# Grouping the part-array matmuls of a two-layer graph network kernel into two stretches per group

## The chip, the core and the metric

The kernel runs on one core of a Trainium2 chip. Five engines work beside each other, each through its own list of instructions in order: TensorE (PE; its weight loads are shown as PEld), VectorE (DVE), ScalarE (ACT), GpSimd (POOL) and SyncE (SP), which here only starts DMAs. ScalarE and GpSimd start DMAs as well. Engines wait for each other through semaphores. The metric is the device time of one execution in microseconds (us).

## The reference

Two layers over a batch of 128 graphs, each with 128 nodes and 512 features; everything is float32.

```python
# layer 0: h = relu(layernorm(x))
q, k, v = h @ Wq.T, h @ Wk.T, h @ Wv.T
rel = adjacency.T[None] * einsum('bnd,bmd->bnm', q, k)
rel = rel / norm(rel, axis=2, keepdims=True)
x = x + einsum('bnm,bmd->bnd', rel, v)
# layer 1: h = relu(layernorm(x)), 8 heads of 64
q, k, v = (h @ Wq + bq), (h @ Wk + bk), (h @ Wv + bv)      # as [b, n, 8, 64]
scores = einsum('bihd,bjhd->bhij', q, k) / 8 + where(adj == 0, -1e9, 0)
x = x + einsum('bhij,bjhd->bihd', softmax(scores), v)
```

## The kernel before

The batch is cut into 32 groups of four graphs (numbered 0 to 3 in a group). A group goes through layer 0, then layer 1. Layer 0 needs two products with weights (G, in which Wq and Wk are merged, and V), layer 1 three (Q, K, V). Each is a (512 x 512) by (512 x 512) product done by Strassen's scheme in the form with seven multiplications, and class `Product` holds its seven steps P1 to P7. One step is eight matmul passes on TensorE (`mm`, L225) into one of three PSUM banks x, y, z, and then one operation that takes the result out of the bank: `keep` or `copy` on ScalarE (on VectorE for layer 1's V), `add` on VectorE. P6, P7 and P4 add onto bank x, and P3 onto bank z, so each waits until the step before it has been copied out of that bank.

All engines follow an order written out by hand: lists of steps (`FIRST`, `SECOND`, `ORDER`, `LAST`) which `run` goes through. `ORDER` is used for thirty of the groups. The letter ahead of the point says whose step it is: `l` is layer 1 of the group in work, `m` layer 0 of the next, `n` layer 1 of that next group, `f` layer 0 of the one after, `p` layer 1 of the group before `l`. So while `l` is multiplied, `m` and the rest of `p` run beside it. Each step appends instructions to the lists of the engines it uses; an engine never does a later step's instruction ahead of an earlier one's.

The steps that the change touches:

- `S(b)` (L459): the scores of graph b, eight heads of 64 rows each, so a matmul uses half of the array's rows and two run side by side. They go to the two banks `pss` (pool `ps_s`) or, for b = 1, to two banks `pso` of pool `ps_o`. `mk(b)` adds the mask and takes the negative row maximum on VectorE (L484, L489); `ex(b)` does eight exponentials on ScalarE and sends the weights to a scratch buffer in DRAM (L191). `mkA`, `mkB`, `exC`, `exD` are the same in two halves, for scores that lie in two `pso` banks.
- `wr(b)` fetches the weights back in blocks with four DMAs of SP (L199), `wt(b)` transposes them within blocks on VectorE (L511) and takes the reciprocal of the sums.
- `A(i)` (L619): the outputs of graphs 2i and 2i+1, matmuls that write 64 of the 128 partitions. `oc(i)` copies them out on ScalarE and sends them, `rdo(i)` fetches them, `ot(i)` transposes and scales them and adds them to the output in DRAM with two DMAs of POOL (L661). "First outputs" are A(0), "second outputs" A(1).
- `N` (L411): the norm sums of layer 0, matmuls that write 32 partitions each. They need `mask_rel` (VectorE) and `square` (ScalarE) of the result of `R`.
- `hn(i)` normalises two graphs on ScalarE (L308) and sends them (512 KB), `rd(i)` fetches them with SP, `T(i)` transposes them on VectorE (L320). `T(0)` makes the operand of P1 and P2, `T(1)` and the sums `sumA`, `sumB` those of the other steps.
- `O(b)` and `xO(b)`: layer 0's outputs on TensorE, then scaled and added to x on VectorE; `stat` and `inv` (VectorE, POOL) make the statistics for layer 1's `hn`.
- `load`, `sto`: x comes in (POOL) and goes out (SP).

Part-array matmuls are those of S, N and A; all others use the whole array. Buffers: `tpool` holds two fetched tiles u, `scratch` four DRAM buffers of each kind, `ppool` one tile for tag `pgv`, which gT (from G) and layer 1's v share.

Of the kernel before, what the change touches and what calls it, by code (L numbers as in the profile page):

```python
# [9 lines left out]
F32 = mybir.dt.float32  # L10
# [4 lines left out]
P = 128  # L15
G = 4
# [5 lines left out]
def kernel(  # L22
# [28 lines left out]
    ppool = ctx.enter_context(tc.tile_pool(name="ppool", bufs=1))  # L51
    rpool = ctx.enter_context(tc.tile_pool(name="rpool", bufs=4))
    npool = ctx.enter_context(tc.tile_pool(name="npool", bufs=3))
    tpool = ctx.enter_context(tc.tile_pool(name="tpool", bufs=2))
    wpool = ctx.enter_context(tc.tile_pool(name="wpool", bufs=3))
    work = ctx.enter_context(tc.tile_pool(name="work", bufs=2))
    small = ctx.enter_context(tc.tile_pool(name="small", bufs=8))
    scratch = ctx.enter_context(
        tc.tile_pool(name="scratch", bufs=4, space=bass.MemoryType.DRAM)
    )  # L60
    ps_mm = ctx.enter_context(tc.tile_pool(name="ps_mm", bufs=4, space=PSUM))
    ps_s = ctx.enter_context(tc.tile_pool(name="ps_s", bufs=1, space=PSUM))
# [139 lines left out]
    class Product:  # L202
# [7 lines left out]
            self.bias, self.name, self.ps, self.r = bias, name, {}, {}  # L210

        def quarter(self, i, j):
            if self.turned:
                return self.dest[:, 2 * j : 2 * j + 2, i * HF : (i + 1) * HF]
            return self.dest[:, 2 * i : 2 * i + 2, j * HF : (j + 1) * HF]

        def mm(self, bank: str, w: int, xs, first: bool):
            if first:
# [154 lines left out]
    class Layer0(Layer):  # L373
        n = 0

        def start(self):
            g = self.g
            self.gT = ppool.tile([P, KD, G * P], F32, tag="pgv", name=f"gT_{g}")
            self.v = ppool.tile([P, G, D], F32, tag="pv0", name=f"v0_{g}")
            self.po = {}  # L380
            self.G = Product(self, "a", self.gT, True, name=f"pg_{g}")
            self.V = Product(self, "v0", self.v, False, name=f"pv0_{g}")

        def R(self):

            pr = ps_o.tile([P, G, P], F32, tag="po", name=f"pr_{self.g}")
            for b in range(G):
                for k in range(KD):
                    nc.tensor.matmul(  # L389
                        pr[:, b, :], lhsT=self.turned(k, b), rhs=self.gT[:, k, ts(b, P)],  # L390
                        start=(k == 0), stop=(k == KD - 1),
                    )
            self.pr = pr
# [43 lines left out]
    class Layer1(Layer):  # L437
# [15 lines left out]
                nc.sync.dma_start(out[self.g * G + b], x_tiles.pop((self.g, b)))  # L453

        def start_v(self):
            self.v = ppool.tile([P, G, D], F32, tag="pgv", name=f"v1_{self.g}")
            self.V = Product(self, "v1", self.v, False, bv_sb, name=f"pv1_{self.g}")

        def S(self, b):  # L459
            g = self.g  # L460

            if b == 1 or (b == 3 and g == NG - 1):
                half = [ps_o.tile([P, NH, P], F32, tag="po", name=f"pso_{g}_{r}") for r in range(2)]
            else:
                pss = ps_s.tile([P, 2, NH, P], F32, tag="ps", name=f"pss_{g}_{b}")
                half = [pss[:, r] for r in range(2)]
                self.ps[b] = pss.rearrange("p r k j -> p (r k) j")
            self.half_s[b] = half
            for k in range(NH):
                for r in range(2):  # L470
                    rows = slice(r * HD, (r + 1) * HD)
                    nc.tensor.matmul(  # L472
                        half[r][:, k, :],
                        lhsT=self.qT[rows, k, ts(b, P)], rhs=self.kT[rows, k, ts(b, P)],
                        start=True, stop=True,
                    )
# [94 lines left out]
        def An(self, b):  # L571

            wT, self.po[b] = self.wT.pop(b), []
            parts = 2 if b == G - 1 else 1
            n = NH // parts
            for t in range(parts):
                pool, tag = (ps_mm, "mm") if b % 2 else (ps_o, "po")
                po = pool.tile([P, 2 * n * HD], F32, tag=tag, name=f"pn1_{self.g}_{b}_{t}")
                for k in range(n):
                    for r in range(2):  # L580
                        i = 2 * (t * n + k) + r
                        nc.tensor.matmul(
                            po[:, ts(2 * k + r, HD)], lhsT=wT[:, r * NH + t * n + k, :],
                            rhs=self.v[:, b, ts(i, HD)], start=True, stop=True,
                        )
                self.po[b].append(po)

# [31 lines left out]
        def A(self, i):  # L619


            for b in range(2 * i, 2 * i + 2):
                wT = self.wT.pop(b)
                po = ps_o.tile([P, NH, P], F32, tag="po", name=f"po1_{self.g}_{b}")
                for k in range(NH):
                    for r in range(2):
                        nc.tensor.matmul(  # L627
                            po[r * HD : (r + 1) * HD, k, :],
                            lhsT=self.v[:, b, ts(2 * k + r, HD)], rhs=wT[:, r * NH + k, :],
                            start=True, stop=True,  # L630
                        )
                self.po[b] = po
# [39 lines left out]
    """.split()  # L672
    SECOND = """
        l.Q.P1 l.sumA l.Q.P2 l.sumB l.K.P1 l.K.P2 l.Q.P5 l.Q.P6 l.sto0 l.sto1 f.load0 f.load1 l.Q.P3 l.K.P5 l.K.P6 l.Q.P7
        l.K.P3 l.K.P7 l.S0 l.mk0 f.load2 f.load3 l.Q.P4 l.K.P4 l.ex0 l.wr0 m.V.P1 f.stat0 f.stat1 f.inv0
        m.V.P2 m.V.P5 m.R m.mask_rel m.square f.stat2 f.stat3 f.inv1 m.V.P6 l.S1 m.N l.S2 l.mkA1 m.norms l.exC1
        l.mkB1 l.exD1 l.wr1 l.wt0 m.V.P3 l.add_mask2 m.V.P7 m.O0 m.xO0 m.O1 m.xO1 n.stat0 n.stat1 n.inv0
        m.V.P4 l.mx2 n.hn0 n.rd0 l.exC2 l.exD2 l.wr2 l.start_v l.V.P1 m.O2 m.xO2 m.O3 m.xO3 n.stat2 n.stat3 n.inv1
        l.V.P2 l.wt1 l.V.P5 n.hn1 n.rd1 l.V.P6
        l.V.P3 n.T0 l.V.P7 l.S3 l.A0 l.mk3 l.oc0 l.wt2 l.V.P4 l.ex3 n.T1 n.start  # L680
    """.split()
    ORDER = """
        l.Q.P1 p.rdo0 l.sumA l.Q.P2 p.wr3 m.hn0 l.sumB l.K.P1 m.rd0 l.K.P2 p.ot0 l.Q.P5 l.Q.P6 m.hn1 m.rd1
        l.sto0 l.sto1 l.Q.P3 l.Q.P7 p.wt3 m.T0 l.K.P5 l.K.P6 l.Q.P4 f.load0 f.load1 l.K.P3
        l.K.P7 m.T1 m.sumA m.sumB m.start m.G.P1 l.K.P4 m.G.P2 l.S0 p.A1 l.mk0 p.oc1 p.rdo1 m.G.P5 m.G.P6
        l.ex0 l.wr0 m.G.P3 m.V.P1 m.G.P7 p.ot1 m.V.P2 f.stat0 f.stat1 f.inv0 m.G.P4 m.V.P5
        l.wt0 f.load2 f.load3 m.R m.mask_rel m.square m.V.P6 l.S1 m.N l.S2 l.mkA1 m.norms l.exC1 l.mkB1 l.exD1
        l.wr1 m.V.P3 l.add_mask2 m.V.P7 m.O0 m.xO0 m.O1 m.xO1 n.stat0 n.stat1 n.inv0 m.V.P4 l.mx2
        n.hn0 n.rd0 l.exC2 l.exD2 l.wr2 l.start_v l.V.P1 m.O2 m.xO2 m.O3 m.xO3 n.stat2 n.stat3 n.inv1
        l.V.P2 l.wt1 l.V.P5 n.hn1 n.rd1 l.V.P6 f.stat2 f.stat3 f.inv1  # L690
        l.V.P3 n.T0 l.V.P7 l.S3 l.A0 l.mk3 l.oc0 l.wt2 l.V.P4 l.ex3 n.T1 n.start
    """.split()
    LAST = """
        l.Q.P1 p.rdo0 l.sumA l.Q.P2 p.wr3 l.sumB l.K.P1 l.K.P2 p.ot0 l.Q.P5 l.Q.P6 l.Q.P3 p.wt3 l.K.P5 l.K.P6
        p.A1 p.oc1 p.rdo1 l.K.P3 l.Q.P7 l.S0 l.mk0 l.K.P7 l.ex0 l.wr0 l.Q.P4 p.ot1 l.K.P4 l.S1 l.mkA1 l.exC1
        l.start_v l.V.P1 l.mkB1 l.exD1 l.wr1 l.V.P2 l.wt0 l.V.P5 l.S2 l.S3 l.add_mask2 l.V.P6 l.mx2 l.exA2 l.exB2
        l.mkA3 l.exA3 l.V.P3 l.V.P7 l.tw2 l.wt1 l.mkB3 l.exB3 l.V.P4 l.An0 l.fin0 l.An1 l.fin1 l.tw3 l.An2 l.fin2
        l.An3 l.fin3
    """.split()
# [1 line left out]
    def run(order, **who):  # L701
        for step in order:
            name, *path = step.split(".")
            at = who.get(name)
            if at is None:
                continue
            if len(path) == 2:
                getattr(getattr(at, path[0]), path[1])()
            elif path[0][-1].isdigit():
                getattr(at, path[0][:-1])(int(path[0][-1]))  # L710
            else:
                getattr(at, path[0])()

    with tc.manual_schedule(engines={EN.PE, EN.SP, EN.Pool, EN.DVE, EN.Activation}):
        p, l, m = None, None, Layer0(0)
        for b in range(G):
            m.stat(b)
        m.inv(0)
        m.inv(1)
        for b in range(G):  # L720
            load(1, b, nc.gpsimd)
        load1()
        m.hn_pe(0)
        m.hn_pe(1)
        f = Layer0(1)
        weights0(lambda: m.turn_pe(0))
        m.turn_pe(1)
        weights_v0()
        for g in range(NG):
            n = Layer1(g)  # L730
            if g:
                f = Layer0(g + 1) if g + 1 < NG else None
            run((FIRST, SECOND, ORDER)[min(g, 2)], p=p, l=l, m=m, n=n, f=f, w=Weights1())
            p, l, m = l, n, f
        run(LAST, p=p, l=l)


# [28 lines left out]
```

## Time and profile before

| What | us |
|---|---|
| median of 3 runs (2489.47 to 2493.50) | 2490.89 |
| the profiled execution | 2492.48 |
| its span, from first to last instruction | 2490.6 |
| TensorE's granted clock in the span | 0.999 of full speed |

| one group, 1281.77 to 1358.32 | busy us |
|---|---|
| TensorE matmul | 76.55 of 76.55 |
| TensorE weight load | 65.53 |
| VectorE | 52.48 |
| ScalarE | 31.73 |
| GpSimd | 12.49 |
| DMA engines, mean busy share | 0.64 |

A timeline row gives the start, the length, the engine, the source line, the operation, the tile written and those read, shapes and the number of instructions; in brackets, how long the engine was idle before it and what released it. Matmuls overlap in the pipeline, so rows of TensorE are to be read from start to start and not by their lengths. "ACTq", "SPq" are DMAs that the engine issues. The DMA rows end with the median time in us from issue to landing.

### The profile page before, as it was taken

Reading aid. Unit: us, or ns where it says so; the run is one execution under the profiler, and the core shown is the slowest. Engines: PE = TensorE matmul, PEld = TensorE weight load, DVE = VectorE, ACT = ScalarE, POOL = GpSimd, SP = SyncE. Lnnn points to the kernel's source line nnn. Section 1 sums busy time; section 2 is a strip of 40 time slices with the busy share of each in tenths; the row PEclk is TensorE's granted clock in tenths of the full one; section 3 lists DMA queues with packets and bytes.
Section 4 is the critical chain, followed back from the end, with each engine's and each line's share of the span. In section 5 each row is a group of like instructions: output and inputs, shape, how many; then the busy total and the mean of one; then the engine's idle time right before and its main releaser. Section 6 shows DMA issues by size and latency. Waiting matters only on the chain.

```text
span 2490.6 us, 40700 instructions
## 1 busy us (share of the span) xinstructions
PE 2480.6 (100%) x14688; PEld 2114.1 (85%) x14688; DVE 1686.6 (68%) x2549; ACT 1028.4 (41%) x3248; POOL 417.3 (17%) x820
## 2 busy tenths in 40 slices
PE   9999999999999999999999999999999999999999
PEld 7888888888888888888888888888888888888887
DVE  5666776666766677766677666676667776667766
ACT  3344443444433444434444344443444443344434
POOL 5111111111111111111111111111111111111110
PEclk9999999999999999999999999999999999999999
DMA  5366655676655766556665566665566655666555
GB/s 188 114 182 191 194 164 167 174 196 181 181 167 168 196 182 182 175 162 180 195 186 170 166 173 197 184 169 169 169 196 186 178 169 163 193 192 181 177 146 134
DMA packets 396408, 438.21 MB, mean 176 GB/s; under 512 B 31600, under 2 KB 289008, under 8 KB 396208
## 3 DMA queue, kind: packets, MB, share of 16 engines
q1 hardware_dynamic: 297376, 201.22, 29.8%
q10 hardware_dynamic: 70000, 165.96, 18.2%
q0 software_dynamic: 28832, 68.44, 13.3%
q8 instruction: 116, 1.90, 0.3%
q14 instruction: 84, 0.69, 0.1%
HBM read 204.80 MB, written 230.69 MB: 175 GB/s over the span
## 4 chain that ended last, share of the span: by engine, by line
PE 93%; DMA 2%; DVE 1%; ACT 1%; issue 1%; SPq 0%; POOL 0%; ACTq 0%; DVEq 0%; POOLq 0%
PE pv_x L225 16%; PE pg_x L225 9%; PE pv_z L225 9%; PE pq_x L225 8%; PE pk_x L225 8%; PE pg_z L225 5%; PE pr L389 5%; PE po L627 4%; PE pq_z L225 4%; PE pk_z L225 4%; PE pv_y L225 4%; PE po L429 4%; PE pss L472 4%; PE pg_y L225 2%; PE pk_y L225 2%; PE pq_y L225 2%
## 5 line engine op out<-in xcount | busy, mean ns | idle before, releaser
L225 PE MATMUL pv_x<-wc_v,h 128*128 128x256 f32 x1280 | 300.6, 382 | 0.1
L320 DVE STREAM_TRANSPOSE h<-u_h 128x1024 f32<-128x1024 f32 x126 | 156.8, 1245 | 187.7 <-DMA u_h<-d_h 185.0
L225 PEld LDWEIGHTS pv_x<-wc_v,h 128*128 128x128 f32 x1280 | 240.4, 190 | 50.8 <-issue 19.5
L661 POOL DMA_DIRECT2D out_dram<-o x124 | 111.8, 901 | 1013.5 <-DVE o L654 1010.5
L225 PE MATMUL pv_z<-wc_v,s 128*128 128x256 f32 x1024 | 245.2, 382 | 0.3 <-DVE pv_r L242 0.3
L308 ACT ACTIVATE hn<-xb,shift,rstd 128x512 f32<-128x512 f32 x252 | 191.5, 810 | 74.6 <-POOL shift L300 57.4
L225 PEld LDWEIGHTS pv_z<-wc_v,s 128*128 128x128 f32 x1024 | 191.8, 190 | 29.3 <-DVE pv_r L242 0.7
L496 ACT ACTIVATE e<-pss,nmax 128x128 f32<-128x128 f32 x504 | 177.7, 381 | 42.7 <-DVE nmax L489 42.7
L225 PE MATMUL pv_x<-wc_v,s 128*128 128x256 f32 x768 | 181.7, 379 | 0.0
L225 PE MATMUL pq_x<-h,wc_q 128*128 128x256 f32 x768 | 181.5, 379 | 0.0
L225 PE MATMUL pk_x<-h,wc_k 128*128 128x256 f32 x768 | 181.5, 379 | 0.0
L638 ACT COPY oT<-po 128x512 f32<-128x512 f32 x124 | 72.8, 587 | 259.0 <-PE po L627 181.1
L290 DVE BATCH_NORM_STATS2 st<-xb 128x6 f32<-128x512 f32 x256 | 172.2, 673 | 8.3 <-DMA xb<-in_x_dram 8.3
L511 DVE STREAM_TRANSPOSE wT<-u_w 128x1024 f32<-128x1024 f32 x126 | 152.8, 1213 | 29.2 <-DMA u_w<-d_w 28.5
L225 PEld LDWEIGHTS pk_x<-h,wc_k 128*128 128x128 f32 x768 | 145.8, 190 | 19.9
L225 PEld LDWEIGHTS pq_x<-h,wc_q 128*128 128x128 f32 x768 | 145.8, 190 | 19.9
L225 PEld LDWEIGHTS pv_x<-wc_v,s 128*128 128x128 f32 x768 | 143.3, 190 | 18.4 <-issue 0.2
L70 POOL DMA_DIRECT2D xb<-in_x_dram x124 | 73.3, 593 | 365.7 <-DMA out_dram<-xb 227.8
L225 PE MATMUL pq_z<-s,wc_q 128*128 128x256 f32 x512 | 122.0, 381 | 2.5 <-DVE qT L249 2.4
L225 PE MATMUL pg_z<-s,wc_a 128*128 128x256 f32 x512 | 124.1, 385 | 0.0
L225 PE MATMUL pg_x<-h,wc_a 128*128 128x256 f32 x512 | 121.0, 379 | 1.1 <-DVE h L320 1.1
L627 PE MATMUL po<-wT,v 128*64 128x128 f32 x1984 | 122.0, 276 | 0.0
(156 smaller groups left out, 4690.8 us busy)
## 6 DMA issues: line engine op xcount, KB each, us to landing
d_h<-hn ACTq DMA_DIRECT2D x126, 512.0 KB, 4.3
u_h<-d_h SPq DMA_DIRECT2D x504, 128.0 KB, 3.6
d_w<-e ACTq DMA_DIRECT2D x126, 512.0 KB, 3.1
u_w<-d_w SPq DMA_DIRECT2D x504, 128.0 KB, 3.4
out_dram<-xb SPq DMA_DIRECT2D x126, 256.0 KB, 3.2
xb<-in_x_dram POOLq DMA_DIRECT2D x124, 256.0 KB, 3.0
d_o<-oT ACTq DMA_DIRECT2D x62, 512.0 KB, 3.8
u_o<-d_o SPq DMA_DIRECT2D x248, 128.0 KB, 3.2
```

What stands on the lines that cost most here:

```text
L70: queue.dma_start(xb, x[g * G + b])
L225: nc.tensor.matmul(ps[:, m, :], lhsT=lhsT, rhs=rhs, start=first and m == 0 and k == 0, stop=k == 1, skip_group_check=True,)
L290: nc.vector.bn_stats(st, x_tiles[g, b])
L308: nc.scalar.activation(hn[:, r], x_tiles[g, b].rearrange("p (k j q) -> p j k q", j=TB, q=BK), AF.Relu, bias=self.shift[:, b : b + 1], scal ...
L320: nc.vector.transpose(half.rearrange("p k (t i) -> p t k i", i=BK), self.u.pop(i).rearrange("p t (k q) -> p t k q", q=BK),)
L389: nc.tensor.matmul(pr[:, b, :], lhsT=self.turned(k, b), rhs=self.gT[:, k, ts(b, P)], start=(k == 0), stop=(k == KD - 1),)
L429: nc.tensor.matmul(po, lhsT=self.rel[:, b, :], rhs=self.v[:, b, :], start=True, stop=True)
L472: nc.tensor.matmul(half[r][:, k, :], lhsT=self.qT[rows, k, ts(b, P)], rhs=self.kT[rows, k, ts(b, P)], start=True, stop=True,)
L496: nc.scalar.activation(e[:, :, i, :], sc[:, i, :].rearrange("p (j q) -> p j q", q=BK), AF.Exp, bias=nmax[:, i : i + 1], accum_out=self.tot ...
L511: nc.vector.transpose(self.wT[b].rearrange("p h (t i) -> p t h i", i=BK), self.uw.pop(b).rearrange("p t (h q) -> p t h q", q=BK),)
L627: nc.tensor.matmul(po[r * HD : (r + 1) * HD, k, :], lhsT=self.v[:, b, ts(2 * k + r, HD)], rhs=wT[:, r * NH + k, :], start=True, stop=True,)
L661: nc.gpsimd.dma_start(out[g * G + b], o.rearrange("p k t q -> p (k t q)"), accum_op=ALU.add)
```

## The change

The part-array matmuls of a group stood in three places: S0 with the second outputs of the group before; S1, N and S2; S3 with the first outputs. They now stand in two: second outputs (A1), S0, S1, N; and S2, S3, first outputs (A0). For that

- S3 uses two `pso` banks in every group, and its mask and exponentials come in halves at the start of the next group (`p.mkA3 p.mkB3 p.exC3 p.exD3`); scores 2 take the place at the group's end (`l.mk2`, `l.exC2 l.exD2 l.wr2`), scores 0 come behind scores 1;
- the outputs go to banks of `ps_mm` instead of `ps_o`;
- gT and layer 1's v are cut into halves, with three half buffers for both, since v's second half now lives until after R of the next group;
- V's steps come in the order P1, P2, P6, then (behind the stretch) P5, P7, P3, P4, and V.P4 stands ahead of O0;
- the fetch and the last step of the second outputs (`o.rdo1`, `o.ot1`) come a group later, so a group before `p` is kept as `o`; `tpool` has three buffers and `scratch` eight;
- `wr0` stands right ahead of `n.rd0`, `rdo0` behind `oc0`, and `f.load2 f.load3` with the statistics earlier.

```diff
-    tpool = ctx.enter_context(tc.tile_pool(name="tpool", bufs=2))
+    tpool = ctx.enter_context(tc.tile_pool(name="tpool", bufs=3))
...
-        tc.tile_pool(name="scratch", bufs=4, space=bass.MemoryType.DRAM)
+        tc.tile_pool(name="scratch", bufs=8, space=bass.MemoryType.DRAM)
...
         def quarter(self, i, j):
-            if self.turned:
-                return self.dest[:, 2 * j : 2 * j + 2, i * HF : (i + 1) * HF]
-            return self.dest[:, 2 * i : 2 * i + 2, j * HF : (j + 1) * HF]
+            a, c = (j, i) if self.turned else (i, j)
+            if isinstance(self.dest, list):
+                return self.dest[a][:, :, c * HF : (c + 1) * HF]
+            return self.dest[:, 2 * a : 2 * a + 2, c * HF : (c + 1) * HF]
...
-            self.gT = ppool.tile([P, KD, G * P], F32, tag="pgv", name=f"gT_{g}")
+            self.gT = [
+                ppool.tile([P, 2, G * P], F32, tag="pgv", bufs=3, name=f"gT_{g}_{j}") for j in range(2)
+            ]
...
-            self.v = ppool.tile([P, G, D], F32, tag="pgv", name=f"v1_{self.g}")
+            self.v = [
+                ppool.tile([P, 2, D], F32, tag="pgv", bufs=3, name=f"v1_{self.g}_{i}") for i in range(2)
+            ]
...
-            if b == 1 or (b == 3 and g == NG - 1):
+            if b % 2:
                 half = [ps_o.tile([P, NH, P], F32, tag="po", name=f"pso_{g}_{r}") for r in range(2)]
...
         def A(self, i):
+            pool, tag = (ps_o, "po") if i and self.g == NG - 2 else (ps_mm, "mm")
             for b in range(2 * i, 2 * i + 2):
                 wT = self.wT.pop(b)
-                po = ps_o.tile([P, NH, P], F32, tag="po", name=f"po1_{self.g}_{b}")
+                po = pool.tile([P, NH, P], F32, tag=tag, name=f"po1_{self.g}_{b}")
...
     ORDER = """
-        l.Q.P1 p.rdo0 l.sumA l.Q.P2 p.wr3 m.hn0 l.sumB l.K.P1 m.rd0 l.K.P2 p.ot0 l.Q.P5 l.Q.P6 m.hn1 m.rd1
-        l.sto0 l.sto1 l.Q.P3 l.Q.P7 p.wt3 m.T0 l.K.P5 l.K.P6 l.Q.P4 f.load0 f.load1 l.K.P3
-        l.K.P7 m.T1 m.sumA m.sumB m.start m.G.P1 l.K.P4 m.G.P2 l.S0 p.A1 l.mk0 p.oc1 p.rdo1 m.G.P5 m.G.P6
-        l.ex0 l.wr0 m.G.P3 m.V.P1 m.G.P7 p.ot1 m.V.P2 f.stat0 f.stat1 f.inv0 m.G.P4 m.V.P5
-        l.wt0 f.load2 f.load3 m.R m.mask_rel m.square m.V.P6 l.S1 m.N l.S2 l.mkA1 m.norms l.exC1 l.mkB1 l.exD1
-        l.wr1 m.V.P3 l.add_mask2 m.V.P7 m.O0 m.xO0 m.O1 m.xO1 n.stat0 n.stat1 n.inv0 m.V.P4 l.mx2
-        n.hn0 n.rd0 l.exC2 l.exD2 l.wr2 l.start_v l.V.P1 m.O2 m.xO2 m.O3 m.xO3 n.stat2 n.stat3 n.inv1
-        l.V.P2 l.wt1 l.V.P5 n.hn1 n.rd1 l.V.P6 f.stat2 f.stat3 f.inv1
-        l.V.P3 n.T0 l.V.P7 l.S3 l.A0 l.mk3 l.oc0 l.wt2 l.V.P4 l.ex3 n.T1 n.start
+        l.Q.P1 p.mkA3 l.sumA m.hn0 l.Q.P2 p.mkB3 p.exC3 l.K.P1 l.sumB m.rd0 p.exD3 p.wr3 l.K.P2 p.ot0 l.Q.P5 p.wt2 l.Q.P6
+        m.hn1 m.rd1 l.sto0 l.sto1 l.Q.P3 l.Q.P7 m.T0 l.K.P5 l.K.P6 p.wt3 l.Q.P4 o.rdo1 f.load0 f.load1 l.K.P3
+        l.K.P7 m.T1 m.sumA m.sumB m.start m.G.P1 l.K.P4 m.G.P2 f.load2 f.load3 m.V.P1 m.G.P5 m.G.P6 o.ot1
+        m.G.P3 f.stat0 f.stat1 f.inv0 m.G.P7 m.V.P2 f.stat2 f.stat3 f.inv1 m.G.P4 m.V.P6 m.R m.mask_rel p.A1 m.square
+        l.S0 p.oc1 l.S1 m.N l.mkA1 m.norms m.V.P5 l.exC1 l.mkB1 m.V.P7 l.exD1 l.wr1 l.add_mask0 m.V.P3 l.mx0
+        m.V.P4 l.ex0 l.wr0 m.O0 m.xO0 m.O1 m.xO1 n.stat0 n.stat1 n.inv0 n.hn0 n.rd0 l.start_v l.V.P1 m.O2 m.xO2 m.O3 m.xO3
+        n.stat2 n.stat3 n.inv1 l.V.P2 l.V.P5 n.hn1 n.rd1 l.wt1 l.V.P6
+        l.V.P3 l.wt0 l.V.P7 n.T0 l.S2 l.S3 l.A0 l.mk2 l.oc0 l.rdo0 l.V.P4 l.exC2 l.exD2 l.wr2 n.T1 n.start
     """.split()
```

`SECOND` (one group) has the same two stretches, without the steps of `p` and `o`. `LAST` (layer 1 of the last group) gets the steps of scores 3 at its start and puts A1 next to S0:

```diff
     LAST = """
-        l.Q.P1 p.rdo0 l.sumA l.Q.P2 p.wr3 l.sumB l.K.P1 l.K.P2 p.ot0 l.Q.P5 l.Q.P6 l.Q.P3 p.wt3 l.K.P5 l.K.P6
-        p.A1 p.oc1 p.rdo1 l.K.P3 l.Q.P7 l.S0 l.mk0 l.K.P7 l.ex0 l.wr0 l.Q.P4 p.ot1 l.K.P4 l.S1 l.mkA1 l.exC1
...
+        l.Q.P1 l.sumA l.Q.P2 p.mkA3 l.sumB l.K.P1 p.exC3 p.mkB3 l.K.P2 p.exD3 p.wr3 p.ot0 l.Q.P5 o.rdo1 l.Q.P6 p.wt2 l.Q.P3
+        l.K.P5 l.K.P6 l.K.P3 p.wt3 l.Q.P7 p.A1 l.S0 p.oc1 p.rdo1 o.ot1 l.mk0 l.K.P7 l.ex0 l.wr0 l.Q.P4 p.ot1 l.K.P4 l.S1 l.mkA1 l.exC1
...
```

## The prediction

> **What bounds the kernel now.** The page's table of engines comes first, then the chain that ended last.
>
> ```profile
> PE 2480.6 (100%) x14688; PEld 2114.1 (85%) x14688; DVE 1686.6 (68%) x2549; ACT 1028.4 (41%) x3248; POOL 417.3 (17%) x820
> PE 93%; DMA 2%; DVE 1%; ACT 1%; issue 1%; SPq 0%; POOL 0%; ACTq 0%; DVEq 0%; POOLq 0%
> ```
>
> TensorE is never without work, so its own order and pace are the time. The groups repeat, so I read one on the timeline, from Q.P1 at 1203.85 us to the next at 1281.77. I call the start of Q.P1 zero. Q.P1 of the third group starts at 129.61 and that of the last stage at 2432.06: thirty groups in 2302.45, 76.75 each. The commonest length, with no wait in it, is 76.55. So waits cost 0.20 a group (late sums or transposes before Q.P5 and G.P1), and TensorE's own work is 76.55.
>
> TensorE's rows around one part-array stretch, and two neighbouring score blocks that the last stage already has:
>
> ```profile
> 1229.39 1.89 PE L225 MATMUL pk_x<-h,wc_k 128*128 128x256 f32 x8
> 1231.12 1.89 PE L225 MATMUL pg_y<-h,wc_a 128*128 128x256 f32 x8
> 1232.94 1.16 PE L472 MATMUL pss<-kT,qT 64*128 64x128 f32 x16
> 1234.03 1.97 PE L627 MATMUL po<-wT,v 128*64 128x128 f32 x32
> 1235.93 1.99 PE L225 MATMUL pg_z<-s,wc_a 128*128 128x256 f32 x8
> 1237.76 1.89 PE L225 MATMUL pg_x<-s,wc_a 128*128 128x256 f32 x8
> ...
> 2466.18 1.16 PE L472 MATMUL pss<-kT,qT 64*128 64x128 f32 x16
> 2467.18 1.06 PE L472 MATMUL pso<-kT,qT 64*128 64x128 f32 x16
> 2468.16 1.99 PE L225 MATMUL pv_x<-wc_v,s 128*128 128x256 f32 x8
> ```
>
> Read start to start. A product takes 1.73; one followed by a stretch 1.82 (1231.12 to 1232.94); one that follows a stretch 1.83 (1235.93 to 1237.76). Scores alone take 1.09, outputs A 1.90, norms N 0.36 (1256.33 to 1256.69). Two score blocks in a row take 1.98, not 2.18: a change of shape costs about 0.1 on each side of the border.
>
> ScalarE at the start of a group:
>
> ```profile
> 1203.60 0.37 ACT L496 ACTIVATE e<-pss,nmax 128x128 f32<-128x128 f32 x1 [0.88 <-DVE nmax L489]
> ...
> 1206.54 0.34 ACTq L191 DMA_DIRECT2D d_w<-e  x1
> 1206.93 0.84 ACT L236 ACTIVATE pq_r<-pq_x,bq_sb 128x256 f32<-128x256 f32 x2 [0.42 <-ACT e L496]
> 1207.65 1.51 ACT L308 ACTIVATE hn<-xb,shift,rstd 128x512 f32<-128x512 f32 x2
> 1209.20 0.37 ACTq L191 DMA_DIRECT2D d_h<-hn  x1
> 1209.61 0.84 ACT L236 ACTIVATE pk_r<-pk_x,bk_sb 128x256 f32<-128x256 f32 x2 [0.44 <-PE pk_x L225]
> 1212.68 0.84 ACT L236 ACTIVATE pq_r<-pq_z,bq_sb 128x256 f32<-128x256 f32 x2 [2.23 <-PE pq_z L225]
> ```
>
> Eight exponentials and their send, Q.P1's copy, the pair hn0 and its send, K.P1's copy, then Q.P5's copy, for which ScalarE waited 2.23 us on TensorE. Its average of 41% hides that this stretch is nearly full.
>
> **The change, part by part.**
>
> *Fewer borders.* Before, a group has S0+A, S1+N+S2 and S3+A: 3 x 0.09 into them, 4 x 1.09, 2 x 1.90, 0.36, 3 x 0.10 out: 9.09. After (compiled order): A,S0,S1,N and S2,S3,A: 2 x 0.09, 2 x 1.98, 2 x 1.90, 0.36, 2 x 0.10: 8.50. That is 0.59 less, a floor of 75.96. A product to A is not new: the last stage has it at 2445.87, 2447.69 and 2449.59, 1.82 and 1.90 again.
>
> [...]
>
> *Scores 3 move into the next group's start.* Before, A waited on S3 next to it, and p.mk3 and p.ex3 ran at the group's end; now p.mk2 and exC2/exD2 run there, and p.mkA3, mkB3, exC3, exD3 follow in the next group. Nothing is computed twice, but ScalarE now has sixteen exponentials before Q.P5's copy instead of eight. Q.P3 adds onto the PSUM bank z that Q.P5 filled, so TensorE cannot start it before that copy (L258, L264). Queued behind Q.P3 is everything that TensorE has, so each late microsecond is one of the group. The chain:
>
> 1. O0 to the group's end: 20.43 before (1261.34 to 1281.77). V.P4 moves ahead of O0 (-1.73) and S2 comes in (1.98-1.09 = +0.89): 19.59.
> 2. O0 to the send of the first half, through xO, the statistics, POOL and hn0: 7.56 (1261.34 to 1268.90), the same steps in the same order: send at -12.03.
> 3. Send to transpose n.T0 (the lag): 8.27 in this group, between 8.3 and 9.2 over thirty groups, middle one 8.54.
>
> ```profile
> 1268.90 0.38 ACTq L191 DMA_DIRECT2D d_h<-hn  x1
> 1271.75 2.04 SPq L199 DMA_DIRECT2D u_h<-d_h  x4
> 1277.17 1.25 DVE L320 STREAM_TRANSPOSE h<-u_h 128x1024 f32<-128x1024 f32 x1 [0.69 <-DMA u_h<-d_h]
> d_h<-hn ACTq DMA_DIRECT2D x126, 512.0 KB, 4.3
> ```
>
> 4. T0 to the first exponential of scores 2: 1.17 to the next VectorE instruction, 1.25 mask, 1.22 maximum, 0.04: 3.68.
> 5. ScalarE without a gap: 2.94 (eight exponentials) + 0.39 + 0.72 (Q.P1) + 1.55 (hn0) + 0.41 + 1.40 (exC3) + 0.72 (K.P1) + 1.54 (exD3) + 0.40 + 0.84 (Q.P5) = 10.91; the four-exponential times are those of scores 1 (1257.94, 1259.49, send 1261.03). And 0.05 to TensorE.
>
> With a lag of 8.54 the copy is done at -12.03+8.54+3.68+10.96 = 11.15. Q.P3 is due after six products, at 10.36. So even with the lag of before it is 0.79 late, which pays back all of the 0.59 and the 0.20.
>
> The lag itself is not kept. Wr0 now stands on SP just ahead of n.rd0, and its fetch is in flight while the 512 KB of hn0 are sent; before, this send went alone and SP saw it landed after 2.85. Sends into a running fetch are in the trace too: the other half of the layer-1 input (7.44 before the group's end) took some 4 to 5.7, and m.hn0 beside the fetch of u_o 4.1 to 4.4. A send of 4.2 makes the lag 9.9. The page's median of all such sends, 4.3, says the same. Lower end: 2.85 + 1.5 of issues + 3.6 (median landing of u_h) = 7.95, if the fetch also gains because scores 2 no longer send at that moment. I take 9.2, between the lag of before and the crowded one, because the two overlap only in part: Q.P3 1.45 late.
>
> [...]
>
> *What else moves.* The second half: send at -8.3; its path before took 9.7 to 12.2, 10.5 in the middle, so n.T1 at 1.4 to 2.3, seldom 3.9. Then mkA3 and the sums stand before Q.P2's add: 1.17+0.73+0.61+0.73+0.61+0.68 = 4.53, so 5.9 to 6.8 against Q.P5 at 6.91. Covered, but nearly used up; a later one falls into the same wait at Q.P3. mk3 in two halves costs VectorE 2 x 1.34 instead of 2.40, beside TensorE. *At nothing:* A into the banks of ps_mm (its successors Q.P2, K.P1 and V.P5 wait for oc, done 1 us or more before); S1 into the other two banks (mask_rel is done 2 us before); gT and v1 in three half buffers, three fetch buffers, eight scratch buffers (space, no instruction); o.rdo1 and l.rdo0 on SP, four issues of some 0.45 each, SP idle from 22.5 to 35.7 before (they would cost if n.rd1 stood behind them; it stands ahead); f.load2/f.load3 earlier on POOL and o.ot1 with its two output DMAs a group later (POOL idles 10.6 and 16.6 us in front of these; the loads need 3.0 and the statistics come over 4 later); wt0 just before A (data about 1 us early, A would pay if the fetch took that longer); m.square before oc (0.6 of ScalarE, V.P5 has 2 us left).
>
> *Ends.* The second group gains 0.59, too. The last stage joins A and S0 (-0.2) and gets the same exponentials ahead of Q.P5's copy without hn0 (0 to +1.7): +0.6 taken. Together nothing.
>
> **Sum.** Thirty groups x (75.96 + late - 76.75). At 1.45 late: 30 x 0.66 = +20. The profiled execution took 2492.48 with a span of 2490.6; the runs' median is 2490.89, so I add to that: **2511 us**.
>
> **Rivals.**
> - *A, faster:* the traffic that leaves (scores 2's send and fetch, before beside this fetch) outweighs the one that comes. Place: n.rd0. Lag 7.95: late 0.20, 30 x (0.20-0.79) = -18, 2473; with no wait at all, 2467. Decides below a lag of 8.38. For it: u_h's median. Against: not one of thirty lags under 8.27.
> - *B, no change:* the lag stays near 8.54; late 0.79, 2491. For it: these lags spread little. Against: wr0 beside it.
> - *C, slower by another wait:* n.T1 comes as late as its worst, 12.2 after its send, at 3.9; the second maximum of scores 3 then comes 5.84 later, at 9.75, and with 1.54+0.40+0.84 the copy ends at 12.5: 2.2 late, 2533. Against: wr2 no longer stands on SP before n.rd1, as it did.
> - That the change does not do what it says is excluded by the compiled order.
>
> **How the numbers follow.** Forecast 0.52, A 0.22, B 0.16, C 0.10. The measurement tells about 0.2% (5 us) from no change; B's bound is a late time of 0.62 to 0.96, lags of 8.38 to 8.72. Slower 0.62, same 0.16, faster 0.22. The likeliest case alone spans 2496 to 2531 (lags 8.72 to 9.9). The whole range goes from 2478, which leaves out the better half of A, to 2531.
>
> **What would show it.** Right: two stretches of 8.50 in all; TensorE idle or a long Q.P6 in front of Q.P3 with ScalarE's copy of pq_z as releaser, about 1.4 a group; a gapless ScalarE from zero to 11; n.T0 later than 2.8 us before the group's end. Wrong: no wait at Q.P3; T0 earlier than 3.6 before the end; or borders that still cost when scores stand together.

## The result and the profile after

| | before | after |
|---|---|---|
| median, us | 2490.80 | 2566.43 |
| lowest to highest | 2489.47 to 2493.50 (4 runs) | 2563.98 to 2569.95 (4 runs) |
| the profiled execution | 2492.48 | 2568.83 |
| its span | 2490.6 | 2567.0 |
| thirty groups, mean of one | 76.75 | 79.00 |
| shortest group | 76.55 | 77.76 |
| last stage, from its Q.P1 to the end of the span | 58.56 | 67.50 |

The ratio is 1.0303, with a 95% interval of 1.0285 to 1.0321. The kernel became slower, as forecast, but by 75.6 us instead of 20, and the time lies 35 us above the upper end of the forecast's range (2531).

The page of the changed kernel, table of engines and chain:

```profile
PE 2487.1 (97%) x14688; PEld 2124.0 (83%) x14688; DVE 1679.8 (65%) x2611; ACT 1009.1 (39%) x3248; POOL 410.6 (16%) x820
PE 62%; DMA 12%; ACT 11%; DVE 7%; SPq 3%; issue 3%; ACTq 1%; POOL 1%; DVEq 0%; POOLq 0%
```

TensorE's busy time has grown by 6.5 us only, while the span has grown by 76.4; so most of the loss is idle time, of which TensorE had hardly any before. The chain that ended last says the same in another way: a third of the span now runs through transfers, ScalarE and VectorE.

The view of TensorE's waits (what waited, for what; us in total, times, longest):

```profile
PE pq_z L226 <- ACT pq_r L237: 62.1, 31, 2.8
PE pg_x L226 <- DVE gT L250: 3.8, 5, 1.0
PE pq_x L226 <- DVE h L321: 3.2, 4, 1.0
```

One wait makes up nearly all of it: pq_z for pq_r, which is Q.P3 for Q.P5's copy, once in every group (thirty) and once in the last stage. The timeline shows where it comes from, here around the Q.P1 at 1313.88:

```profile
1301.12 2.27 SPq L199 DMA_DIRECT2D u_w<-d_w  x4
1301.83 0.38 ACTq L191 DMA_DIRECT2D d_h<-hn  x1
...
1306.07 4.26 SPq L199 DMA_DIRECT2D u_h<-d_h  x8
1306.34 1.89 PE L226 MATMUL pv_x<-wc_v,h 128*128 128x256 f32 x8
1308.16 1.16 PE L477 MATMUL pss<-kT,qT 64*128 64x128 f32 x16
1309.16 1.06 PE L477 MATMUL pso<-kT,qT 64*128 64x128 f32 x16
1310.15 1.97 PE L633 MATMUL po<-wT,v 128*64 128x128 f32 x32
...
1311.43 1.25 DVE L321 STREAM_TRANSPOSE h<-u_h 128x1024 f32<-128x1024 f32 x1 [2.29 <-DMA u_h<-d_h]
1312.60 1.20 DVE L489 TENSOR_TENSOR pss<-pss,mask 128x1024 f32<-128x1024 f32 x1
1313.83 1.22 DVE L494 TENSOR_REDUCE nmax<-pss 128x8 f32<-128x1024 f32 x1
1315.09 0.37 ACT L530 ACTIVATE e<-pss,nmax 128x128 f32<-128x128 f32 x1 [2.34 <-DVE nmax L494]
...
1325.19 0.84 ACT L237 ACTIVATE pq_r<-pq_z,bq_sb 128x256 f32<-128x256 f32 x2 [0.42 <-ACT e L530]
1326.08 1.99 PE L226 MATMUL pq_z<-s,wc_q 128*128 128x256 f32 x8 [1.68 <-ACT pq_r L237]
```

Read from start to start, TensorE's own work is as forecast: 1.82 for the product ahead of a stretch, 1.00 and 0.99 for the two score blocks, 1.90 for A. The send of hn0 starts at 1301.83, 12.05 before Q.P1, while the four fetches of `wr0` (1301.12) are being issued. SP has issued these by 1303.4 and then waits for the send: it starts the fetch of h 4.24 after the send. T0 runs 9.60 after the send, the first exponential 3.66 after T0 begins, and Q.P5's copy is done 10.94 after that, with ScalarE never idle by more than 0.50. From T0's start to Q.P3 this row took 14.64 to 14.73 in each of the thirty groups. Q.P3 is due at 1313.88 + 10.36 = 1324.24 and starts at 1326.08. Scores 2 had been in PSUM since about 1309.3: their mask stood behind T0 on VectorE, and T0 stood waiting for a transfer.

Over the thirty groups, what lies above the floor of 75.96, from the starts of TensorE's blocks:

| loss per group | us |
|---|---|
| wait at Q.P3 (Q.P6 to Q.P3 3.87 instead of 1.73) | 2.14 |
| slower product after that wait (1.83 instead of 1.73) | 0.10 |
| TensorE at half clock, 7 groups x 1.68 | 0.39 |
| Q.P5, G.P4 and Q.P1 waiting for VectorE, and small ones | 0.41 |
| sum | 3.04 |

The mean before, 76.75, lies 0.79 above that floor, so 2.25 a group is the loss against before, 67.5 in thirty groups. With 8.9 from the last stage it makes the 76.4 of the spans.

The half clock is new. TensorE at the Q.P3 of 613.21, first in the view by stretches of time (its length, the busy time of PE, PEld, DVE, ACT and POOL with their numbers of instructions, then the granted clock, the DMA share and GB/s), then on the timeline:

```profile
612.60:614.50 1.90, 1.29 (x3) 1.11 (x4) 1.87 (x4) 1.90 (x6) 1.25 (x2) 0.63 0.88 312
614.50:616.50 2.00, 2.00 (x6) 1.55 (x6) 0.62 (x1) 0.79 (x2) 0.56 (x1) 0.50 1.09 219
616.50:620.00 3.50, 3.50 (x18) 3.09 (x17) 2.10 (x3) 0.00 (x0) 0.00 (x0) 1.00 1.10 264
```

```profile
613.21 3.61 PE L226 MATMUL pq_z<-s,wc_q 128*128 128x256 f32 x8 [2.17 <-ACT pq_r L237]
616.66 1.89 PE L226 MATMUL pq_x<-h,wc_q 128*128 128x256 f32 x8
```

After a wait of 2.17 the clock is at 0.50 for 3.41 us (613.11 to 616.52), and the eight matmuls take 3.45 from start to start instead of 1.73.

The last stage of the changed kernel, TensorE and one row of VectorE:

```profile
2512.82 1.99 PE L226 MATMUL pq_z<-s,wc_q 128*128 128x256 f32 x8 [2.81 <-ACT pq_r L237]
2529.78 1.99 PE L226 MATMUL pk_x<-h,wc_k 128*128 128x256 f32 x8 [1.31 <-DVE kT L250]
2534.87 0.71 DVE L655 STREAM_TRANSPOSE o<-u_o 128x512 f32<-128x512 f32 x1 [5.14 <-DMA u_o<-d_o]
2540.63 0.49 PE L477 MATMUL pso<-kT,qT 64*128 64x128 f32 x2 [1.29 <-ACT e L530]
2542.57 2.07 PE L477 MATMUL pso<-kT,qT 64*128 64x128 f32 x14 [1.45 <-ACT e L530]
2544.57 3.78 PE L226 MATMUL pv_x<-wc_v,s 128*128 128x256 f32 x8
```

Four waits, 6.9 us together, on TensorE. S3 (`pso`) waits for the exponentials of scores 1, whose masks stand behind `p.ot1` on VectorE, and that stands 5.14 us for the fetch of the outputs. Then half clock again: 0.50 from 2541.64 for 6.83 us.

### The profile page after: what moved, and what is told of

It is laid out like the page before. It is cut to its first block, busy times and chain, and to the rows that moved or that the text cites. A ratio compares the mean times of both kernels' runs of the same rounds, so it can differ in the third digit from the quotient of the medians.

```text
span 2567.0 us, 40544 instructions
## 1 busy us (share of the span) xinstructions
PE 2487.1 (97%) x14688; PEld 2124.0 (83%) x14688; DVE 1679.8 (65%) x2611; ACT 1009.1 (39%) x3248; POOL 410.6 (16%) x820
## 4 chain that ended last, share of the span: by engine, by line
PE 62%; DMA 12%; ACT 11%; DVE 7%; SPq 3%; issue 3%; ACTq 1%; POOL 1%; DVEq 0%; POOLq 0%
PE pv_x L226 10%; PE pg_x L226 8%; ACT e L530 6%; PE pv_z L226 6%; PE pk_x L226 5%; PE pr L392 4%; DMA d_h<-hn 4%; DMA u_h<-d_h 4%; PE pq_x L226 4%; PE pg_z L226 4%; PE pk_z L226 3%; PE po L432 3%; PE po L633 3%; PE pv_y L226 3%; ACT hn L309 3%
## 5 line engine op out<-in xcount | busy, mean ns | idle before, releaser
L226 PE MATMUL pv_x<-wc_v,h 128*128 128x256 f32 x1280 | 305.8, 382 | 0.0
L226 PE MATMUL pq_z<-s,wc_q 128*128 128x256 f32 x512 | 132.7, 405 | 62.9 <-ACT pq_r L237 62.1
L530 ACT ACTIVATE e<-pso,nmax 128x128 f32<-128x128 f32 x504 | 178.6, 386 | 23.1 <-DVE pso L547 13.8
L226 PEld LDWEIGHTS pq_z<-s,wc_q 128*128 128x128 f32 x512 | 97.8, 197 | 91.5 <-ACT pq_r L237 74.5
L547 DVE TENSOR_TENSOR pso<-pso,mask 128x512 f32<-128x512 f32 x128 | 87.1, 680 | 95.5 <-PE pso L477 95.5
L655 DVE STREAM_TRANSPOSE o<-u_o 128x512 f32<-128x512 f32 x124 | 87.4, 705 | 76.0 <-DMA u_o<-d_o 76.0
```

Of the source, the lines that this page charges most:

```text
L226: nc.tensor.matmul(ps[:, m, :], lhsT=lhsT, rhs=rhs, start=first and m == 0 and k == 0, stop=k == 1, skip_group_check=True,)
L530: nc.scalar.activation(e[:, :, i, :], sc[:, k, :].rearrange("p (j q) -> p j q", q=BK), AF.Exp, bias=nmax[:, i : i + 1], accum_out=self.tot ...
L547: nc.vector.tensor_tensor(sc, sc, mask[:, None, :].to_broadcast([P, NH, P]), ALU.add)
L655: nc.vector.transpose(o.rearrange("p k t q -> p t k q"), u[:, n * TB : (n + 1) * TB].rearrange("p t (k q) -> p t k q", q=BK),)
```

## The experiments

Each is the changed kernel with the edit shown. Times are medians, compared with the kernel before on the same chip.

**1. Half of the exponentials of scores 3 behind Q.P5's copy.** In `ORDER` only:

```diff
-        l.Q.P1 p.mkA3 l.sumA m.hn0 l.Q.P2 p.mkB3 p.exC3 l.K.P1 l.sumB m.rd0 p.exD3 p.wr3 l.K.P2 p.ot0 l.Q.P5 p.wt2 l.Q.P6
+        l.Q.P1 p.mkA3 l.sumA m.hn0 l.Q.P2 p.mkB3 p.exC3 l.K.P1 l.sumB m.rd0 l.K.P2 p.ot0 l.Q.P5 p.wt2 l.Q.P6 p.exD3 p.wr3
```

> The changed kernel with one step moved: the second half of scores 3's exponentials (exD3, with its send and wr3) stands behind the copies of Q.P5 and Q.P6 on ScalarE instead of ahead of them; nothing else differs. Theory (the wait at Q.P3 is ScalarE's own row of work since the transpose T0): the copy of Q.P5 comes 1.94 us earlier (1.54 of exponentials and 0.40 of the send), so the wait in front of Q.P3 falls from 2.1 us to 0.2 to 0.4 a group, no half-clock window is left behind it, and the time falls from 2566 to about 2495 to 2510 (30 x 2.2 less, some of it given back later). Rival (the wait comes from something else that ends at the same time, such as a sum of VectorE, which waits for T1): it stays above 1.5 us a group and the time above 2550.

Measured: 2556.21, ratio 1.0253 (1.0236 to 1.0271). The waits of TensorE:

```profile
PE pk_x L226 <- DVE kT L250: 45.7, 31, 2.1
PE pq_z L226 <- ACT pq_r L237: 7.0, 14, 2.3
```

The wait at Q.P3 goes from 62.1 to 7.0, so it was indeed ScalarE's full row. But the time missed the forecast by far, because K.P4 now waits for kT in every group:

```profile
1331.77 1.25 DVE L516 STREAM_TRANSPOSE wT<-u_w 128x1024 f32<-128x1024 f32 x1 [5.97 <-DMA u_w<-d_w]
...
1333.51 0.67 DVE L250 TENSOR_TENSOR kT<-pk_x,pk_r 128x512 f32<-128x512 f32 x1
...
1334.24 1.99 PE L226 MATMUL pk_x<-h,wc_k 128*128 128x256 f32 x8 [1.05 <-DVE kT L250]
```

The weights of scores 3 are sent later, their transpose `p.wt3` stands on VectorE for them, and the sum of K.P7 stands behind it. The work that was moved out of one path stands in another, and the wait moves with it.

**2. T0 behind the mask of scores 2.** In `ORDER` and `SECOND`:

```diff
-        l.V.P3 l.wt0 l.V.P7 n.T0 l.S2 l.S3 l.A0 l.mk2 l.oc0 l.rdo0 l.V.P4 l.exC2 l.exD2 l.wr2 n.T1 n.start
+        l.V.P3 l.wt0 l.V.P7 l.S2 l.S3 l.A0 l.mk2 l.oc0 n.T0 l.rdo0 l.V.P4 l.exC2 l.exD2 l.wr2 n.T1 n.start
```

> The changed kernel with one step moved: VectorE does the mask and maximum of scores 2 (mk2) ahead of the transpose T0 instead of behind it. Theory (T0, which waits for its DMAs until 2.1 us before the group's end, starts ScalarE's row late): the exponentials of scores 2 can start about 0.6 us before the group's end instead of 1.6 behind it, held then by the copies of the first outputs; the wait at Q.P3 goes to 0 to 0.2 us a group and the time to 2475 to 2500. Rival (ScalarE's row is late for another reason than T0, or the DMAs of the group's start come later too and hold it): the wait stays above 1 us and the time above 2530.

Measured: 2491.94 (ten runs, 2489.01 to 2498.92), ratio 1.0007 (0.9997 to 1.0016), 74 us less than after. VectorE and ScalarE on the timeline around the Q.P1 at 1665.40, then TensorE's waits:

```profile
1660.89 1.23 DVE L489 TENSOR_TENSOR pss<-pss,mask 128x1024 f32<-128x1024 f32 x1 [0.34 <-PE pss L477]
1662.16 1.22 DVE L494 TENSOR_REDUCE nmax<-pss 128x8 f32<-128x1024 f32 x1
1663.30 1.25 DVE L321 STREAM_TRANSPOSE h<-u_h 128x1024 f32<-128x1024 f32 x1
...
1664.77 0.37 ACT L530 ACTIVATE e<-pss,nmax 128x128 f32<-128x128 f32 x1 [0.50 <-DVE h L321]
```

```profile
PE pg_x L226 <- DVE gT L250: 9.6, 14, 2.2
PE pq_x L226 <- DVE h L321: 3.9, 7, 0.8
PE pq_z L226 <- ACT pq_r L237: 0.6, 1, 0.6
```

The mask now starts as soon as scores 2 are there, and in this group T0 follows without a wait. The exponentials start 0.63 ahead of Q.P1 instead of 1.21 behind it, and Q.P3 waits in none of the thirty groups (the one wait of 0.6 lies outside them), although T0 still comes as late behind its send as after the change (10.04 in the middle). The bracket of the exponentials names T0 because it ended last before them; they do not need it: ahead of the Q.P1 at 668.29 T0 ran until 0.19 before Q.P1, and they started at the same 0.63. The shortest group is 76.00, the floor that the borders promised (75.96). The mean is 76.70: G.P4 now waits for gT, and Q.P1 for T0 (0.15 a group). The last stage, not edited, is still 65.81. These lengths are of the profiled execution, 2498.92, which is the longest of the ten and 7 us above the median.

**3. Both edits together.**

> Both moves together. Theory: no wait at Q.P3 is left, nor a half clock behind it, and what the fewer borders give comes out: 30 x 0.59 = 18 us less than before from the groups, so a group near 75.96 to 76.3 and 2475 to 2490, with about 8 us still lost in the last stage, which is not touched. Rival (the grouping has a cost of its own, in the banks, the halves or the later fetch of outputs): groups stay above 76.75 and the time above 2495.

Measured: 2528.87, ratio 1.0146 (1.0127 to 1.0164): the expectation was missed, and the groups (77.54 in the mean) did stay above 76.75. But the waits name another cause than the grouping itself:

```profile
PE pk_x L226 <- DVE kT L250: 36.6, 31, 2.6
DVE wT L516 <- DMA u_w<-d_w: 208.6, 57, 8.5
```

The second line is VectorE's: it waits 208.6 us for weights, against 103.0 in experiment 2. With T0 out of the way the first edit is of no use any more, and its price at K.P4 stays (45.7 us in experiment 1, 36.6 here).

**4. Without the fetch of the weights of scores 0.** All groups but the last use these weights as ScalarE wrote them, without the exchange between blocks:

```diff
+            if b == 0 and self.g < NG - 1:
+                self.dw.pop(b)
+                self.uw[b] = self.e.pop(b).rearrange("p j h q -> p j (h q)")
+                return
```

> The changed kernel without the fetch of scores 0's weights (wr0, four DMAs of 128 KB in each group but the last); the transpose wt0 reads the exponentials in place, so these weights are left as they are before the exchange of blocks. Theory (this fetch is in flight beside the send of hn0 and makes the lag 9.95 instead of 8.5): the lag falls to 8.4 to 8.8, the wait at Q.P3 from 2.1 to about 0.8 to 1.0 us a group, and with fewer half-clock windows the time falls to 2515 to 2535. Rival (the lag is longer for another reason, such as the second half's send 3.5 us behind the first instead of 5.4): the lag stays above 9.5 and the time above 2555.

Measured: 2514.83, ratio 1.0086 (1.0061 to 1.0111). The same half of the layer-1 input as above, and TensorE's first wait:

```profile
1277.82 0.38 ACTq L191 DMA_DIRECT2D d_h<-hn  x1
1280.68 6.36 SPq L199 DMA_DIRECT2D u_h<-d_h  x8
...
1286.11 1.25 DVE L321 STREAM_TRANSPOSE h<-u_h 128x1024 f32<-128x1024 f32 x1 [1.09 <-DMA u_h<-d_h]
```

```profile
PE pq_z L226 <- ACT pq_r L237: 26.7, 31, 2.3
```

SP starts the fetch 2.86 after the send, as before the change (2.85), and no longer 4.24. T0 follows 8.29 after the send, and the wait at Q.P3 is 1.01 a group in the mean. The second half is still sent 3.5 behind the first, so that rival falls; the time ends just below the range. Over thirty groups, middle values:

| from the send of hn0 | before | after | without wr0 |
|---|---|---|---|
| to the start of its fetch | 2.89 | 4.08 | 2.86 |
| from there to T0 | 5.62 | 5.95 | 5.57 |
| the lag | 8.54 | 9.94 | 8.45 |

So `wr0` beside the send is what lengthened the lag, by about 1.2 in the send and 0.3 in the fetch; about half of the wait came from it, and the other half was there at the old lag.

**5. Experiment 2, with o.ot1 later.** In `ORDER`, from ahead of G.P3's copy to ahead of G.P4:

```diff
-        l.K.P7 m.T1 m.sumA m.sumB m.start m.G.P1 l.K.P4 m.G.P2 f.load2 f.load3 m.V.P1 m.G.P5 m.G.P6 o.ot1
-        m.G.P3 f.stat0 f.stat1 f.inv0 m.G.P7 m.V.P2 f.stat2 f.stat3 f.inv1 m.G.P4 m.V.P6 m.R m.mask_rel p.A1 m.square
+        l.K.P7 m.T1 m.sumA m.sumB m.start m.G.P1 l.K.P4 m.G.P2 f.load2 f.load3 m.V.P1 m.G.P5 m.G.P6
+        m.G.P3 f.stat0 f.stat1 f.inv0 m.G.P7 m.V.P2 f.stat2 f.stat3 f.inv1 o.ot1 m.G.P4 m.V.P6 m.R m.mask_rel p.A1 m.square
```

> T0 back behind the second mask add, and o.ot1 moved in the hand-written order from ahead of G.P3's copy to behind the statistics (ahead of G.P4). Theory: the wait that remains in the run with T0 back (0.40 to 0.49 us per group at G.P4, on VectorE's gT) comes from o.ot1 standing on VectorE, waiting for its fetch, ahead of the adds of G.P3 and G.P7. Then the groups' mean falls from 76.70 to 76.15 to 76.35 (what is left is Q.P1's wait for T0, 0.15, and the switch's tenths), and the time to 2474 to 2482; the last stage is unchanged at 65 to 67.5. Rival: the adds of G.P3 and G.P7 are late for another reason (T1's product terms on VectorE), so the wait stays and the time is 2489 to 2494; or the transposes now hold mask_rel or the second layer's masks and the time is above 2494.

Measured: 2479.71, ratio 0.9951 (0.9936 to 0.9966). The mean group is 76.13. The wait for gT, 9.6 us in experiment 2, is out of TensorE's waits. There it looked like this:

```profile
1621.70 0.71 DVE L655 STREAM_TRANSPOSE o<-u_o 128x512 f32<-128x512 f32 x1 [3.54 <-DMA u_o<-d_o]
...
1627.33 1.99 PE L226 MATMUL pg_x<-h,wc_a 128*128 128x256 f32 x8 [0.24 <-DVE gT L250]
```

So it was `o.ot1`, standing on VectorE for its fetch ahead of two sums that G.P4 needs. The medians of the two experiments differ by 12 us, the thirty groups of the two profiled executions by 17, since the long execution was profiled in experiment 2. These are the waits for tiles with more than 0.7 us that are left in the groups and the last stage:

```profile
PE pso L477 <- ACT e L530: 2.9, 2, 1.5
...
PE pk_x L226 <- DVE kT L250: 1.2, 2, 1.1
PE po L633 <- DVE wT L516: 1.1, 1, 1.1
PE pq_x L226 <- DVE h L321: 0.8, 3, 0.5
```

All but the last line and 0.1 of kT's 1.2 lie in the last stage, which is still 65.32.

**6 and 7. The last stage, on top of experiment 5.** The sixth issues `o.rdo1` first, and puts `o.ot1` and `p.ot1` elsewhere in `LAST`; the seventh puts `p.ot1` into another gap. The sixth against the fifth:

```diff
-        l.Q.P1 l.sumA l.Q.P2 p.mkA3 l.sumB l.K.P1 p.exC3 p.mkB3 l.K.P2 p.exD3 p.wr3 p.ot0 l.Q.P5 o.rdo1 l.Q.P6 p.wt2 l.Q.P3
-        l.K.P5 l.K.P6 l.K.P3 p.wt3 l.Q.P7 p.A1 l.S0 p.oc1 p.rdo1 o.ot1 l.mk0 l.K.P7 l.ex0 l.wr0 l.Q.P4 p.ot1 l.K.P4 l.S1 l.mkA1 l.exC1
-        l.start_v l.V.P1 l.mkB1 l.exD1 l.wr1 l.V.P2 l.wt0 l.V.P5 l.S2 l.S3 l.add_mask2 l.mx2 l.exA2 l.exB2 l.V.P6
+        o.rdo1 l.Q.P1 l.sumA l.Q.P2 p.mkA3 l.sumB l.K.P1 p.exC3 p.mkB3 l.K.P2 p.exD3 p.wr3 p.ot0 l.Q.P5 l.Q.P6 p.wt2 l.Q.P3
+        l.K.P5 o.ot1 l.K.P6 l.K.P3 p.wt3 l.Q.P7 p.A1 l.S0 p.oc1 p.rdo1 l.mk0 l.K.P7 l.ex0 l.wr0 l.Q.P4 l.K.P4 l.S1 l.mkA1 l.exC1
+        l.start_v l.V.P1 l.mkB1 l.exD1 l.wr1 l.V.P2 l.wt0 l.V.P5 l.S2 l.S3 l.add_mask2 l.mx2 p.ot1 l.exA2 l.exB2 l.V.P6
```

and the seventh against the sixth:

```diff
-        l.start_v l.V.P1 l.mkB1 l.exD1 l.wr1 l.V.P2 l.wt0 l.V.P5 l.S2 l.S3 l.add_mask2 l.mx2 p.ot1 l.exA2 l.exB2 l.V.P6
+        l.start_v l.V.P1 l.mkB1 l.exD1 l.wr1 l.V.P2 p.ot1 l.wt0 l.V.P5 l.S2 l.S3 l.add_mask2 l.V.P6 l.mx2 l.exA2 l.exB2
```

> The run before it and, in the last stage alone, o.rdo1 issued first, o.ot1 moved between the keys' fifth and sixth step (VectorE idles 4.5 us there), and p.ot1 moved from ahead of the masks of scores 1 to behind those of scores 2. Theory: in the last stage p.ot1 holds VectorE 4.84 us for its fetch while the masks of scores 1 wait, so that scores 3 wait 1.0 + 1.45 for the exps of scores 1, and the half-speed clock that follows (6.83 us) costs about 3.4 more; o.ot1 ahead of mk0 costs 1.2 at K.P4. Without them the last stage falls from 65.8 to 58.5 to 61 us and the time is 5 to 7.5 us below the run before. Rival: the last stage is longer by the part of group 31's scores 2 and 3 that now lies in it and by their exps, so it stays within 1.5 us of 65.8 and the time within 2 us.

Measured: 2477.66, ratio 0.9943 (0.9927 to 0.9960), 2 us below the fifth, and a last stage of 62.83: the theory's 58.5 to 61 missed. The waits for S3, K.P4 and most of A1's were gone, but a new one stood in their place:

```profile
PE pv_x L226 <- DVE pv_r L243: 3.0, 1, 3.0
```

I had put `p.ot1` ahead of V.P6's copy, on which TensorE waits; half clock followed this wait, too: 3.41 us of it, and the product took 3.49 from start to start (2457.67 to 2461.16) instead of 1.73. The seventh:

> The run before it (2477.66), but in the last stage p.ot1 stands behind the sum of V.P2, where VectorE idled 1.77 us for the weights of scores 0, and V.P6's copy ahead of the maximum of scores 2. Theory: the 3.02 us that TensorE waited for pv_r there, and the 3.41 us of half clock after it (1.7 us of time), came from p.ot1's four instructions (2.7 us) standing ahead of V.P6's copy. Then the last stage falls from 62.8 to 58.5 to 60.5 and the time to 2473.5 to 2475.5. Rival: the output's fetch has not landed there (the gap is only 1.77 us wide), so p.ot1 holds V.P5's copy and the masks of scores 2 instead, the wait only moves, and the time stays at 2476.5 to 2480.

Measured: 2474.40 (2473.80 to 2476.53), ratio 0.9937 (0.9921 to 0.9954), and a last stage of 58.84. Its table of engines, its chain and all of TensorE's waits for tiles:

```profile
PE 2462.8 (100%) x14688; PEld 2114.6 (86%) x14688; DVE 1684.0 (68%) x2611; ACT 1014.1 (41%) x3248; POOL 418.5 (17%) x820
PE 96%; DMA 2%; DVE 1%; issue 0%; POOL 0%; ACT 0%; SPq 0%; ACTq 0%; DVEq 0%; POOLq 0%
```

```profile
PE pq_x L226 <- DVE h L321: 2.3, 4, 0.9
...
PE pq_z L226 <- ACT pq_r L237: 0.6, 1, 0.6
PE pg_x L226 <- ACT pg_r L234: 0.2, 1, 0.2
```

TensorE is busy for 100% of the span again, and its work is 17.8 us less than before (2480.6). This version is 17 us faster than the kernel before and 92 us faster than the changed one, with the same two stretches: thirty groups at 76.13 instead of 76.75 save 18.5, and the last stage costs 0.3.

## Why the prediction was wrong

The direction, the place of the wait and four of the five steps of its chain were right. The third step, the lag, was not: it was taken as 9.2 and was 9.9 in the middle. And several terms that the sum had at nothing were not nothing. 20 were forecast for the whole, and the spans differ by 76.4. Term by term, with the losses counted from the floor of 75.96 as in the forecast:

| term | forecast, us | measured, us |
|---|---|---|
| own work of thirty groups against the mean before | -23.7 | -23.7 |
| late at Q.P3, thirty groups | 43.5 | 64.2 |
| slower product after the wait | 0 | 3.0 |
| half clock in seven groups | 0 | 11.8 |
| Q.P5, G.P4, Q.P1 and small ones | 0 | 12.3 |
| second group, last stage, the rest | 0 | 8.8 |
| sum | 19.8 | 76.4 |

With the measured lag the sum would have given 2533: 21 of the 57 us that were missed are the lag, and 36 are the terms at nothing.

- *Borders.* Right, 0.59 a group was nearly the size: the shortest groups of the runs without the wait took 76.00 to 76.02, which is 0.53 to 0.55 less than the shortest before.
- *Steps 1, 2, 4 and 5 of the chain.* Right: the send at -12.05 (forecast -12.03), T0 to the exponentials 3.66 (3.68), ScalarE's gapless row 10.94 (10.91), and 0.05 from there to TensorE.
- *Step 3, the lag.* This is the step of the chain that failed: "I take 9.2, between the lag of before and the crowded one, because the two overlap only in part". The middle lag was 9.94, with 9.4 to 11.8 around it, as long as the crowded value of 9.9. The overlap was not partial: in the group shown the four fetches of `wr0` landed 1.8 to 5.4 after the send was issued, and the send itself after 4.2, so the fetch ran beside the whole of the send. The send took 3.1 to 4.5 (as SP saw it; 4.08 in the middle), like the crowded rows, not halfway, and without `wr0` it took 2.86 (experiment 4). Each tenth of the lag costs 3 us. In five groups T0 came so late (1.39 ahead of Q.P1) that Q.P1 itself waited for it, which the prediction did not have. The crowded sends of before were read as 4 to 5.7; one of the thirty took 6.4 (the middle landing was 4.3).
- *A wait was priced by its length alone.* The half clock after seven of these waits and the slower product after each add 15 us. In the thirty groups before, TensorE waited 1.13 at the longest, and no half clock followed, so no row showed the one. The other could be read there: the products that the three waits of more than 0.3 at Q.P5 (0.31 to 1.07) held back took 1.83.
- *"At nothing": o.ot1 a group later.* GpSimd's idle time was named as its cover. But the step also stands on VectorE for its fetch, ahead of the sums for G.P4. In the changed kernel this wait is small (3.8 us in all), mostly hidden behind the larger one; in experiment 2, where that is gone, it is 9.6.
- *The sums behind n.T1.* "Covered, but nearly used up" was right in kind: T1 ran at 1.5 to 2.8 and Q.P5 waited a tenth of a us per group. It followed V.P4's copy without a gap there; its path was VectorE and not, as I had it, the transfer.
- *Ends.* "+0.6 taken" for the last stage, 8.9 measured. I counted the border and the exponentials ahead of Q.P5, but not that A1 now starts 22.2 after Q.P1 (2521.65) instead of 15.6; only 3.0 of this is the wait at Q.P3. So its outputs are fetched later, and `p.ot1`, which waits for them, holds the masks of scores 1. Without the wait at Q.P3 the last stage still took 65.81 (experiment 2). Experiments 6 and 7 show that the place of the three steps is the rest: 58.84 with them moved, against 65.32.
- *The rivals.* B had its lag in experiment 4 (T0 mostly 8.3 to 8.5 behind the send) and gave 2514.83, not 2491: even the kept lag would have been slower, most of it by the terms that were at zero (the last stage alone took 64.82 instead of 58.56). A and C did not occur: no lag was below 9.4, and Q.P5's copy was not set by T1.
- *What was not asked.* The chain was taken as given. The mask of scores 2 needs nothing from T0; it waited only because the hand-written order had T0 ahead of it. This one place is worth 74 us, more than everything that the change moves on TensorE.

## What to carry to other kernels

When a step that feeds the critical engine is queued behind one that waits for a transfer, price the transfer's lag as its crowded rows show it, and ask first whether the two have to stand in that order. Price an idle stretch of TensorE with what follows it, and not by its length alone. When work is moved, look for every in-order queue on which its waiting instruction stands, and in the stages at the ends of the loop, too: here a few steps on VectorE, in the wrong places, made a loss of 3% out of a gain of 0.6%.

## What the runs showed of the hardware

- Half clock after short waits. In the changed kernel TensorE's clock fell to 0.50 for 3.41 us at seven of the thirty waits at Q.P3, and for 6.83 us in the last stage; six of the seven cost 1.69 and one 1.62. The length of a wait alone does not decide: one of 2.05 was followed by it and one of 2.33 was not. At these waits its place decided. The eight stretches start at 613.11, 773.54, 1169.48, 1483.51, 1643.93, 2193.48, 2432.41 and 2541.64, and every distance between them is a whole multiple of 3.4133 (47, 116, 92, 47, 161, 70 and 32 times, to within 0.01 us). So in this run the clock changed on a grid of 3.4133 us. Cut along this grid, the seven waits had 2.05 to 2.31 of their idle time in one cell, and half clock filled the next cell; the other waits at Q.P3 had at most 1.99 in one cell (of the 2.81 in the last stage 1.90). In the last stage it followed two waits of 1.29 and 1.45 with two score matmuls between them, of which 1.8 fell in one cell; so the idle time in a cell did not decide alone, either. In two other runs a product after waits took about twice its 1.73 from start to start: 3.49 in experiment 6, after one of 3.02 (2457.67 to 2461.16), and 3.57 in the last stage of experiment 2, with 14 score matmuls after waits of 1.00 and 1.45 ahead of it (2474.73 to 2478.30).
- A 512 KB send to DRAM had landed 2.9 after its issue when alone (the kernel before, 1268.90 to 1271.75; experiment 4, 1277.82 to 1280.68) and 4.2 beside a fetch of the same size (the changed kernel, 1301.83 to 1306.07), as seen by the queue that waited for it; 3.1 to 4.5 over thirty groups of the changed kernel.
